# Edge loop of a graph network: four rotating one-bank PSUM tiles in place of two two-bank tiles

## The chip, the cores and the metric

The kernel runs on one core of a Trainium2 chip. The metric is the device time of one execution, in microseconds (us); the median of three runs before the change is 1214.6 us. The engines are named as in the profile: PE is TensorE (PEld its weight loads), DVE is VectorE, ACT is ScalarE, POOL is GpSimd and SP is SyncE.

## What is computed

One layer of message passing over 6250 nodes of 128 features and 100000 edges that are sorted by destination, then a residual and a layer norm:

```python
row, col = (edge_index[0], edge_index[1])
msg_in = jnp.concatenate([node_features[row], node_features[col]], axis=-1)
h = jax.nn.relu(msg_in @ Wm1 + bm1)
h = jax.nn.relu(h @ Wm2 + bm2)
messages = h @ Wm3 + bm3
agg = jax.ops.segment_sum(messages, col, num_segments=num_nodes)
count = jax.ops.segment_sum(jnp.ones((messages.shape[0],), messages.dtype), col, num_segments=num_nodes)
agg = agg / jnp.clip(count, 1.0)[:, None]
node_in = jnp.concatenate([node_features, agg], axis=-1)
upd = jax.nn.relu(node_in @ Wn1 + bn1) @ Wn2 + bn2
...
x = _layernorm(x + _L0_gnn_ref(...), axis=-1)
```

## The kernel before

It has three stages. The first makes two tables in device memory, one row a node: `atab`, the source half of the first product, in float32, and `btab`, the destination half, in three bfloat16 terms. The second, the edge loop, is nearly the whole time. The third applies the node network and the norm.

The edge loop takes the edges in groups of 512 (four tiles of 128), two groups at a time: 196 groups, so 98 pairs. Each group's destinations fall into few nodes, so a one-hot product over a narrow window of nodes sums them. A pair passes through these parts, which overlap with those of its neighbours (in step p of the loop, different pairs are at different parts):

- `fetch`: POOL issues eight indirect gathers of `atab` rows into the tile `rows` (L437); SP issues the loads of the `btab` windows (L443). `rows` has two buffers, so the gathers of pair p+2 wait until the first layer of pair p has read its own.
- `make_hot`: DVE builds one-hot tiles, `oht` (L461) and `oh` (L464).
- `first_layer`: PE transposes the gathered rows (L478) and adds the destination terms (L485) into the tile `ph`, which takes four of the eight PSUM banks; ACT makes `h1` of it (L491).
- `second_layer`: PE multiplies `h1` by `w2` (L499), eight matmuls a group; DVE takes the maximum with the negated bias into `h2` (L503), in one instruction of 128x1024 for the first group of a pair and two of 128x512 for the second (`cuts`). The bias itself is added later, per node.
- `sums`: PE multiplies the one-hot tiles by `h2`, which gives a sum per node of each window (L511); `part_of` copies it to SBUF on ACT (L519; L522 for the short last pair).
- `turned` and `add_up`: PE transposes these sums (L533), and DVE adds each window, 21 nodes wide, into the accumulator `acc` at an offset that it reads at run time (L542), eight adds a pair.

The order on PE, ACT and DVE is the order in which the code is written (`manual_schedule`). In step p PE runs `turned` of pair p-3, `first_layer` of p, `sums` of p-2 and `second_layer` of p-1. DVE runs `add_up` of p-3, `make_hot` of p+1 and the maxima of p-1. ACT runs the activations of p and the copy of p-2. In a few steps a piece of other work is put between: some blocks of the node part (`x_part`, L327, with evictions L329 and L331) in the first two steps and the last but one, and a doubling of the inputs (L567 on DVE, with its loads and stores on SP).

The other four PSUM banks are the pool `p2`. Everything but the first layer takes its tile there. A tile is two banks and there are two of them:

```python
def banks():
    return p2.tile([P, 2, 2 * H], F32, name="banks")

def bank():
    return banks()[:, 0, :].rearrange("p (t h) -> p t h", t=2)
```

One step takes four such tiles: `pt` in `turned`, `pg` in `sums`, and `ph2` twice in `second_layer`. Whoever takes a tile waits until the last reader of the tile that had the buffer before is done with all of it, and a reader waits until all that was written to its tile, in the region that it reads or in the same banks, is there. Which buffer a tile gets is settled when the program is built.

Of the kernel before, what the change touches and what calls it, by code (L numbers as in the profile page):

```python
# [19 lines left out]
P = 128  # L20
EPS = 1e-5
NONE = 16384
WN = 32
# [4 lines left out]
def kernel(  # L28
# [121 lines left out]
    with tc.tile_pool(name="prep", bufs=1) as prep, tc.tile_pool(  # L150
# [183 lines left out]
        def whole(steps):  # L334
            for _ in steps:
                pass
# [75 lines left out]

    with edge, tc.tile_pool(name="wk", bufs=2) as wk, tc.tile_pool(
        name="p1", bufs=1, space=PSUM
    ) as p1, tc.tile_pool(name="p2", bufs=2, space=PSUM) as p2:


        NH2 = 2
# [1 line left out]
        for t in h2s:  # L420
            nc.vector.memset(t[:, :, H:], 1.0)

        def banks():
            return p2.tile([P, 2, 2 * H], F32, name="banks")

        def bank():
            return banks()[:, 0, :].rearrange("p (t h) -> p t h", t=2)

        def fetch(groups):

# [22 lines left out]
        def hot(groups):  # L453


            ohts = wk.tile([P, 2, 2, P], BF16, name="oht")
            ohs = []
            for i, (db, pb_cols, dl, nt) in enumerate(groups):
                n = nt * WN
                for k in range(2):  # L460
                    nc.vector.tensor_scalar(ohts[:n, i, k, :], db[:n, k * P:(k + 1) * P], pb_cols[:n, k:k + 1], None,  # L461
                                            op0=ALU.is_equal)
                oh = wk.tile([P, GT, WN], F32, name="oh", bufs=6)
                nc.vector.tensor_tensor(oh[:, :nt, :], iota_n.to_broadcast([P, nt, WN]),  # L464
                                        dl.rearrange("p (j o) -> p j o", o=1).to_broadcast([P, nt, WN]),
                                        op=ALU.is_equal)
                ohs.append(oh)
            return ohts, ohs
# [23 lines left out]
                                         ph[:, i, :nh, c, :], AF.Relu, bias=b1[:, c:c + 1])  # L492
            return h1

        def second_layer(h1, h2, nt, cuts):
            ph2 = banks().rearrange("p b (t h) -> p (b t) h", t=2)
            for j in range(nt):
                for c in range(HC):
                    nc.tensor.matmul(ph2[:, j, :], h1[:, c, j * P:(j + 1) * P],  # L499
                                     w2[:, c, :], start=(c == 0), stop=(c == HC - 1))  # L500
            step = nt // cuts
            for j in range(0, nt, step):
                nc.vector.tensor_tensor(h2[:, j:j + step, :H], ph2[:, j:j + step],  # L503
                                        nb2.to_broadcast([P, step, H]), op=ALU.max)

        def sums(groups):

            pg = banks()
            for i, (oh, h2, nt) in enumerate(groups):
                for j in range(nt):  # L510
                    nc.tensor.matmul(pg[j * WN:(j + 1) * WN, i, :H + 1], oh[:, j, :], h2[:, j, :],  # L511
                                     start=True, stop=True, skip_group_check=True)
            return pg

        def part_of(pg, nts):
            part = wk.tile([P, 2, H + 1], F32, name="part")
            if min(nts) == GT:
                n = len(nts)
                nc.scalar.copy(part[:, :n], pg[:, :n, :H + 1])  # L519
            else:  # L520
                for i, nt in enumerate(nts):
                    nc.scalar.copy(part[:nt * WN, i], pg[:nt * WN, i, :H + 1])  # L522
            return part

        def turned(part, nts):

            pt = banks()[:, :, :2 * (HC + 1) * NQ].rearrange("p h (g c q) -> p h g c q", g=2, q=NQ)
            for i, nt in enumerate(nts):
                for c in range(HC + 1):
                    for h in range(nt // 2):  # L530
                        rows = (part[halves[h], i, c * P:(c + 1) * P] if c < HC
                                else part[halves[h], i, H:].to_broadcast([NQ, P]))
                        nc.tensor.matmul(pt[:, h, i, c, :], rows, ident[halves[h], halves[h]], is_transpose=True,  # L533
                                         start=True, stop=True, skip_group_check=True)
            return pt

        def add_up(pt, firsts, nts):
            for i in reversed(range(len(nts))):
                for j in reversed(range(nts[i])):
                    window = acc[:, :, ds(firsts[i][j], WB)]  # L540
                    k = j % 2 * WN
                    nc.vector.tensor_add(window, window, pt[:, j // 2, i, :, k:k + WB])  # L542
                    yield

        def load_bases(ap, n, engine):
            _, firsts = nc.values_load_multi_w_load_instructions(
# [42 lines left out]
        for i in range(NP + 4):  # L589
            if i == 8:  # L590
                late_loads()

                none = wk.tile([16, (NG * GE - E) // 16 + 1], I32, name="none", bufs=1)
                nc.vector.memset(none, NONE)
                nc.sync.dma_start(dpad[E - 16:].rearrange("(p e) -> p e", p=16), none)
                nc.sync.dma_start(dpad[:E].rearrange("(p e) -> p e", p=16), dst.rearrange("(p e) -> p e", p=16))
            if i < NP:
                dbs = early.pop(0) if early else destinations(2 * i, min(2, NGF - 2 * i), dst_row)
                if 2 * i + 1 == NGF:
                    dbs = dbs + last_destinations()  # L600
                got = fetch([(srcT[:, 2 * i + k, :], firsts) for k, firsts in enumerate(bases(i, ENG.SP))])
                st[i] = dict(nts=NTS[2 * i:2 * i + 2], got=got, dbs=dbs)
            p = i - 1
            if p < 0:
                continue
            if p == 0:
                make_hot(0)
            k = p - 3
            firsts = bases(k, ENG.DVE) if k >= 0 else None
            if k >= 0:  # L610
                pt = turned(st[k]["part"], st[k]["nts"])
                whole(add_up(pt, firsts, st.pop(k)["nts"]))
            for step, after in enumerate((10, 12, 14)):
                if i >= after and (i - after) % 4 == 0 and (i - after) // 4 < len(pieces):
                    double((i - after) // 4, step)
            if p + 1 < NP:
                make_hot(p + 1)
            if p < NP:
                s = st[p]
                s["h1"] = first_layer(s.pop("got"), s.pop("ohts"), s["nts"])  # L620
            if p < 2:
                whole(x_part(X_FIRST[p], bank, (nc.scalar, nc.vector)))
            if p - 2 == NP - 1:
                whole(rest)
            if 0 <= p - 2 < NP:
                st[p - 2]["part"] = part_of(summed(p - 2), st[p - 2]["nts"])
            if 0 <= p - 1 < NP:
                s = st[p - 1]
                for j, nt in enumerate(s["nts"]):
                    second_layer(s["h1"][:, j], h2s[j], nt, 1 + j)  # L630
        assert not st
        turns.close()
        order.close()
# [7 lines left out]
        with tc.For_i(0, groups, 1) as g:  # L641
            more = nc.values_load(
                morei[0:1, ds(g, 1)], min_val=0, max_val=N // 16,
                skip_runtime_bounds_check_because="the difference of two nodes over 16")
            with tc.For_i(0, more, 1):
                for t, by in ((tilei[0:1, ds(g * GT, GT)], float(WB)), (pbase[:, ds(g, 1), :], float(WB)),
                              (dloc[:, ds(g, 1), :], -float(WB))):
                    nc.vector.tensor_scalar(t, t, by, None, op0=ALU.add)
                idx = wk.tile([P, GT], I32, name="idx")
                nc.vector.tensor_copy(idx, srcT[:, ds(g, 1), :].rearrange("p o j -> p (o j)"))  # L650
                pbc = wk.tile([P, 2], F32, name="pbc")
                nc.vector.tensor_copy(pbc, pbase[:, ds(g, 1), :].rearrange("p o k -> p (o k)"))
                dl = wk.tile([P, GT], F32, name="dl")
                nc.vector.tensor_copy(dl, dloc[:, ds(g, 1), :].rearrange("p o j -> p (o j)"))

                ti = wk.tile([1, GT], I32, name="ti")
                nc.vector.tensor_scalar_min(ti, tilei[0:1, ds(g * GT, GT)], float(N - 1))
                got = fetch([(idx, load_bases(ti, GT, ENG.SP))])
                db, = destinations(g, 1, dpad_row)
                ohts, (oh,) = hot([(db, pbc, dl, GT)])  # L660
                h1 = first_layer(got, ohts, [GT])
                second_layer(h1[:, 0], h2s[0], GT, 1)
                part = part_of(sums([(oh, h2s[0], GT)]), [GT])
                whole(add_up(turned(part, [GT]), [load_bases(ti, GT, ENG.DVE)], [GT]))


    NB = 4 * P
# [159 lines left out]
```

## Time and profile before

| | |
|---|---|
| median of 3 runs | 1214.6 us (1214.6 to 1215.05) |
| profiled execution | 1215.59 us; span of its instructions 1213.9 us |
| granted PE clock, mean | 0.992 |
| PE busy | 1139.8 us, 94% of the span |
| POOL busy | 803.9 us (66%), of it 751.6 us in the gathers (L437), 959 ns each |
| DVE busy | 651.5 us (54%) |
| ACT busy | 381.9 us (31%) |
| edge loop, first L499 to last add | 96.1 to 1136.7 us |

The profile shows one execution. Times in a timeline are microseconds from the start of the span: the start, the duration, the engine, the line of the code, the operation, the tiles as output<-input, and in brackets the idle time of the engine before it and what ended that. A row can merge several instructions of a kind (x32). A float32 matmul that is no transpose shows as two records. A waits row gives who waited for whom, the sum in us, how often and the longest.

### The profile page before, as it was taken

The numbers are of one execution on the slowest core, as the hardware profiler recorded it, in microseconds if no ns is written. First come the engines' busy times: TensorE is split into PE (matmuls) and PEld (weight loads), VectorE is DVE, ScalarE is ACT, GpSimd is POOL, SyncE is SP. The second block draws the span as 40 slices with busy tenths as digits, with TensorE's granted clock in tenths as the row PEclk, the third lists the DMA queues.
The fourth block names the chain that finished last, engine by engine and source line by source line (L and its number), as shares of the span: only waits on it lengthen the run. The fifth ranks groups of instructions, "written<-read, shape, count | busy, mean of one in ns | idle before, by whom it ended". The sixth has DMA issues, their size and how long they took to land. (4 is left out here: it accounts for less than half of the span.)

```text
span 1213.9 us, 31892 instructions
## 1 busy us (share of the span) xinstructions
PE 1139.8 (94%) x11196; PEld 909.9 (75%) x11197; DVE 651.5 (54%) x1978; ACT 381.9 (31%) x679; POOL 803.9 (66%) x862
## 2 busy tenths in 40 slices
PE   7989999999999999999999999999999999998897
PEld 6747777787777777877777778777777787776465
DVE  5764455455555555555555544455455444554587
ACT  5753222222222222222222222222222222221256
POOL 5557777777777777777777777777777777770120
PEclk9999999999999999999999999999999999999899
DMA  8776656566565555556655555555555555550243
GB/s 277 277 253 172 172 165 170 156 173 171 151 171 165 162 152 169 171 160 163 168 157 150 156 156 152 154 153 152 146 148 149 153 154 153 153 147 20 84 117 111
DMA packets 173727, 193.61 MB, mean 160 GB/s; under 512 B 30906, under 2 KB 145548, under 8 KB 173548
## 3 DMA queue, kind: packets, MB, share of 16 engines
q0 software_dynamic: 38160, 103.75, 30.7%
q1 hardware_dynamic: 106956, 61.93, 17.5%
q10 hardware_dynamic: 28448, 25.87, 7.3%
q8 instruction: 89, 1.46, 0.5%
q14 instruction: 74, 0.61, 0.2%
HBM read 168.92 MB, written 22.88 MB: 158 GB/s over the span
## 5 line engine op out<-in xcount | busy, mean ns | idle before, releaser
L437 POOL DMA_INDIRECT rows<-atab,srcT x784 | 751.6, 959 | 281.0 <-issue 189.8
L499 PE MATMUL banks<-w,h 128*128 128x256 f32 x3128 | 698.6, 381 | 45.8 <-DVE acc L542 43.0
L499 PEld LDWEIGHTS banks<-w,h 128*128 128x128 f32 x3128 | 586.2, 190 | 165.8 <-PE banks L511 86.2
L503 DVE TENSOR_TENSOR h<-banks,nb 128x512 f32<-128x512 f32 (+1 forms) x294 | 245.7, 864 | 477.3 <-PE banks L499 471.4
L491 ACT ACTIVATE h<-ph,b 128x512 f32<-128x512 f32 x392 | 236.7, 686 | 744.1 <-PE ph L485 728.4
L542 DVE TENSOR_TENSOR acc<-acc,banks 128x63 f32 x782 | 171.6, 219 | 31.8 <-PE banks L533 5.8
L478 PE MATMUL ph<-ident,rows 64*128 64x64 f32 x3128 | 113.8, 223 | 0.6 <-issue 0.6
L478 PEld LDWEIGHTS ph<-ident,rows 64*128 64x128 f32 x3128 | 105.3, 139 | 2.3 <-ACT x_sb L329 1.3
L511 PE MATMUL banks<-h,oh 128*32 128x257 f32 x1564 | 105.3, 386 | 1.0 <-DVE acc L542 1.0
L461 DVE TENSOR_SCALAR oht<-db,pbase 128x128 bf16<-128x128 int32 x392 | 95.7, 291 | 0.2
L708 POOL TENSOR_TENSOR agg<-total,rc 128x512 f32<-128x512 f32 (+2 forms) x15 | 16.0, 1070 | 81.5 <-DMA rcol<-acc 44.4
L533 PEld LDWEIGHTS banks<-ident,part 64*128 64x128 f32 x1173 | 43.3, 137 | 33.2 <-issue 31.8
L485 PE MATMUL ph<-oht,rows 64*128 64x128 bf16 x1564 | 61.1, 216 | 3.4 <-DMA rows<-btab 3.2
L511 PEld LDWEIGHTS banks<-h,oh 128*32 128x32 f32 x1564 | 40.9, 109 | 28.8 <-PE banks L533 1.1
L519 ACT COPY part<-banks 128x514 f32<-128x514 f32 x97 | 58.6, 604 | 9.9 <-PE banks L511 9.9
L533 PE MATMUL banks<-ident,part 64*128 64x64 f32 x1173 | 56.7, 229 | 0.5 <-ACT part L522 0.5
L464 DVE TENSOR_TENSOR oh<-iota_n,dloc 128x128 f32<-128x128 f32 x196 | 55.2, 282 | 0.4 <-PE banks L511 0.4
L235 PE MATMUL pbt<-w,xT 128*128 128x256 f32 x196 | 49.7, 397 | 4.4 <-ACT bt L244 1.7
L485 PEld LDWEIGHTS <-rows 64*128 64x128 bf16 x1564 | 48.9, 95 | 4.2 <-DMA rows<-btab 4.1
L235 PEld LDWEIGHTS pbt<-w,xT 128*128 128x128 f32 x196 | 36.1, 195 | 14.1 <-ACT bt L244 3.5
L703 PE MATMUL pmt<-acc,w 128*128 128x512 f32 (+2 forms) x60 | 26.1, 576 | 3.2 <-DVEq L641 3.2
L731 PEld LDWEIGHTS pot<-wu,u 128*128 128x128 f32 (+1 forms) x196 | 24.0, 191 | 5.1 <-issue 4.5
(112 smaller groups left out, 412.3 us busy)
## 6 DMA issues: line engine op xcount, KB each, us to landing
rows<-btab SPq DMA_DIRECT2D x782, 32.0 KB
db<-in_dst_dram ACTq DMA_DIRECT2D x194, 128.0 KB
rows<-atab,srcT POOLq DMA_INDIRECT x784
btab<-bt SPq DMA_DIRECT2D x24, 384.0 KB
atab<-bt SPq DMA_DIRECT2D x24, 256.0 KB
xd<-in_x_dram SPq DMA_DIRECT2D x12, 256.0 KB
x2tab<-xd SPq DMA_DIRECT2D x12, 256.0 KB
x_sb<-in_x_dram SPq DMA_DIRECT2D x5, 512.0 KB
```

The source lines that it names most:

```text
L235: nc.tensor.matmul(pbt[:, a, :], xT[:, (t0 + a) * P:(t0 + a + 1) * P], w1[:, k, :], start=True, stop=True)
L437: nc.gpsimd.indirect_dma_start(out=ag[:, j, :], out_offset=None, in_=atab[:, :], in_offset=bass.IndirectOffsetOnAxis(ap=idx[:, j:j + 1], a ...
L461: nc.vector.tensor_scalar(ohts[:n, i, k, :], db[:n, k * P:(k + 1) * P], pb_cols[:n, k:k + 1], None, op0=ALU.is_equal)
L478: nc.tensor.matmul(ph[:, i, h, c, u * NQ:(u + 1) * NQ], ag[halves[h], u, c * P:(c + 1) * P], ident[halves[h], halves[h]], is_transpose=Tru ...
L485: nc.tensor.matmul(ph[:, i, h, c, k * P:(k + 1) * P], bw[halves[h], k, c * P:(c + 1) * P], ohts[halves[h], i, k, :], start=False, stop=Tru ...
L491: nc.scalar.activation(h1[:, i, c, :nh * 2 * P].rearrange("p (h e) -> p h e", h=nh), ph[:, i, :nh, c, :], AF.Relu, bias=b1[:, c:c + 1])
L499: nc.tensor.matmul(ph2[:, j, :], h1[:, c, j * P:(j + 1) * P], w2[:, c, :], start=(c == 0), stop=(c == HC - 1))
L503: nc.vector.tensor_tensor(h2[:, j:j + step, :H], ph2[:, j:j + step], nb2.to_broadcast([P, step, H]), op=ALU.max)
L511: nc.tensor.matmul(pg[j * WN:(j + 1) * WN, i, :H + 1], oh[:, j, :], h2[:, j, :], start=True, stop=True, skip_group_check=True)
L519: nc.scalar.copy(part[:, :n], pg[:, :n, :H + 1])
L533: nc.tensor.matmul(pt[:, h, i, c, :], rows, ident[halves[h], halves[h]], is_transpose=True, start=True, stop=True, skip_group_check=True)
L542: nc.vector.tensor_add(window, window, pt[:, j // 2, i, :, k:k + WB])
```

## The change

`p2` gets four buffers of one bank. `second_layer` takes one tile for each two edge tiles, so four a pair, each with a maximum of 128x512 of its own; `sums` takes one tile a group, and ACT copies each group's sums by itself; `turned` takes one tile for each half `h` (which held one bank of the tile before, too), and `add_up` goes through the first half's windows and then the second's, where it went backwards through groups and windows. `oh` gets eight buffers instead of six. The arithmetic is the same; the order of the adds is not. A step now takes eight tiles from four buffers. The lines below L415 move by up to five: L499 becomes L500, L503 L502, L511 L510, L519 and L522 L518, L533 L529 and L542 L539.

```diff
-    ) as p1, tc.tile_pool(name="p2", bufs=2, space=PSUM) as p2:
+    ) as p1, tc.tile_pool(name="p2", bufs=4, space=PSUM) as p2:
...
-        def banks():
-            return p2.tile([P, 2, 2 * H], F32, name="banks")
-
         def bank():
-            return banks()[:, 0, :].rearrange("p (t h) -> p t h", t=2)
+            return p2.tile([P, 2, H], F32, name="bank")
+
+        def flat_bank():
+            return bank().rearrange("p t h -> p (t h)")
...
-                oh = wk.tile([P, GT, WN], F32, name="oh", bufs=6)
+                oh = wk.tile([P, GT, WN], F32, name="oh", bufs=8)
...
-        def second_layer(h1, h2, nt, cuts):
-            ph2 = banks().rearrange("p b (t h) -> p (b t) h", t=2)
-            for j in range(nt):
-                for c in range(HC):
-                    nc.tensor.matmul(ph2[:, j, :], h1[:, c, j * P:(j + 1) * P],
-                                     w2[:, c, :], start=(c == 0), stop=(c == HC - 1))
-            step = nt // cuts
-            for j in range(0, nt, step):
-                nc.vector.tensor_tensor(h2[:, j:j + step, :H], ph2[:, j:j + step],
-                                        nb2.to_broadcast([P, step, H]), op=ALU.max)
+        def second_layer(h1, h2, nt):
+            for j0 in range(0, nt, 2):
+                ph2 = bank()
+                for j in range(j0, j0 + 2):
+                    for c in range(HC):
+                        nc.tensor.matmul(ph2[:, j - j0, :], h1[:, c, j * P:(j + 1) * P],
+                                         w2[:, c, :], start=(c == 0), stop=(c == HC - 1))
+                nc.vector.tensor_tensor(h2[:, j0:j0 + 2, :H], ph2, nb2.to_broadcast([P, 2, H]), op=ALU.max)
 
         def sums(groups):
 
-            pg = banks()
-            for i, (oh, h2, nt) in enumerate(groups):
+            pgs = []
+            for oh, h2, nt in groups:
+                pg = flat_bank()
                 for j in range(nt):
-                    nc.tensor.matmul(pg[j * WN:(j + 1) * WN, i, :H + 1], oh[:, j, :], h2[:, j, :],
+                    nc.tensor.matmul(pg[j * WN:(j + 1) * WN, :H + 1], oh[:, j, :], h2[:, j, :],
                                      start=True, stop=True, skip_group_check=True)
-            return pg
-
-        def part_of(pg, nts):
+                pgs.append(pg)
+            return pgs
+
+        def part_of(pgs, nts):
             part = wk.tile([P, 2, H + 1], F32, name="part")
-            if min(nts) == GT:
-                n = len(nts)
-                nc.scalar.copy(part[:, :n], pg[:, :n, :H + 1])
-            else:
-                for i, nt in enumerate(nts):
-                    nc.scalar.copy(part[:nt * WN, i], pg[:nt * WN, i, :H + 1])
+            for i, (pg, nt) in enumerate(zip(pgs, nts)):
+                nc.scalar.copy(part[:nt * WN, i], pg[:nt * WN, :H + 1])
             return part
 
         def turned(part, nts):
 
-            pt = banks()[:, :, :2 * (HC + 1) * NQ].rearrange("p h (g c q) -> p h g c q", g=2, q=NQ)
+            pts = [flat_bank()[:, :2 * (HC + 1) * NQ].rearrange("p (g c q) -> p g c q", g=2, q=NQ) for _ in range(2)]
             for i, nt in enumerate(nts):
                 for c in range(HC + 1):
                     for h in range(nt // 2):
...
-                        nc.tensor.matmul(pt[:, h, i, c, :], rows, ident[halves[h], halves[h]], is_transpose=True,
+                        nc.tensor.matmul(pts[h][:, i, c, :], rows, ident[halves[h], halves[h]], is_transpose=True,
                                          start=True, stop=True, skip_group_check=True)
-            return pt
-
-        def add_up(pt, firsts, nts):
-            for i in reversed(range(len(nts))):
-                for j in reversed(range(nts[i])):
-                    window = acc[:, :, ds(firsts[i][j], WB)]
-                    k = j % 2 * WN
-                    nc.vector.tensor_add(window, window, pt[:, j // 2, i, :, k:k + WB])
-                    yield
+            return pts
+
+        def add_up(pts, firsts, nts):
+            for h in range(2):
+                for i in range(len(nts)):
+                    for j in range(2 * h, min(2 * h + 2, nts[i])):
+                        window = acc[:, :, ds(firsts[i][j], WB)]
+                        k = j % 2 * WN
+                        nc.vector.tensor_add(window, window, pts[h][:, i, :, k:k + WB])
...
-                    second_layer(s["h1"][:, j], h2s[j], nt, 1 + j)
+                    second_layer(s["h1"][:, j], h2s[j], nt)
```

## The prediction

> **What bounds the kernel now.** I read the page's first part for the engine with the most work, then the waits, then the timeline of one step in the middle, one step near the start and the steps at the end.
>
> ```profile
> PE 1139.8 (94%) x11196; PEld 909.9 (75%) x11197; DVE 651.5 (54%) x1978; ACT 381.9 (31%) x679; POOL 803.9 (66%) x862
> ```
>
> TensorE (PE) is busy for 94% of the span, so the question is what its few idle microseconds wait for. The list of waits answers:
>
> ```profile
> POOL rows L437 <- issue: 189.8, 621, 0.6
> ...
> POOL rows L437 <- PE ph L485: 59.6, 80, 1.0
> ...
> PE banks L499 <- DVE acc L542: 43.0, 94, 0.9
> ```
>
> In 94 of the 98 steps the second layer's first matmul (L499) waits for the last window add of VectorE (DVE, L542), 43.0 us in all: its two-bank tile is the one from which the adds still read. GpSimd (POOL), which gathers rows (L437), waits for PE only 80 times; the rest of its idle time is a fixed 0.30 us between gathers. The timeline of one step (start, duration, engine, line) shows both:
>
> ```profile
> 608.97 0.58 PE L533 MATMUL banks<-ident,part 64*128 64x64 f32 x12
> 609.08 1.29 DVE L503 TENSOR_TENSOR h<-banks,nb 128x512 f32<-128x512 f32 x2 [2.23 <-PE banks L499]
> ...
> 609.39 1.16 PE L478 MATMUL ph<-ident,rows 64*128 64x64 f32 x32
> ...
> 610.28 2.00 DVE L542 TENSOR_TENSOR acc<-acc,banks 128x63 f32 x8
> ...
> 610.38 0.61 PE L485 MATMUL ph<-oht,rows 64*128 64x128 bf16 x16
> ...
> 610.92 1.07 PE L511 MATMUL banks<-h,oh 128*32 128x257 f32 x16
> ...
> 611.27 0.95 POOL L437 DMA_INDIRECT rows<-atab,srcT  x1 [0.78 <-PE ph L485]
> ...
> 612.42 7.14 PE L499 MATMUL banks<-w,h 128*128 128x256 f32 x32 [0.43 <-DVE acc L542]
> ...
> 613.39 0.60 ACT L519 COPY part<-banks 128x514 f32<-128x514 f32 x1
> ...
> 619.50 0.58 PE L533 MATMUL banks<-ident,part 64*128 64x64 f32 x12
> ```
>
> The step lasts 619.50 - 608.97 = 10.53 us. By the starts: L533 to L478 0.42, L478 to L485 0.99, L485 to L511 0.54, L511 to L499 1.50, L499 to the next L533 7.08. The adds start late (610.28) because DVE first does both maxima of the step before, 609.08 to 610.37; and those began only when all eight matmuls of that two-bank tile were done. An early step that has no adds shows the same passage without the wait:
>
> ```profile
> 104.76 1.07 PE L511 MATMUL banks<-h,oh 128*32 128x257 f32 x16
> ...
> 105.76 7.17 PE L499 MATMUL banks<-w,h 128*128 128x256 f32 x32
> ```
>
> L511 to L499 takes 1.00 there, not 1.50. The wait therefore costs 0.50 per step: its 0.43 to 0.46 of idle time and a slower restart.
>
> **The change, part by part.**
>
> *Finer release of the adds' bank.* One step has eight one-bank tiles in four buffers: two for the transposes, two for the sums, four for the second layer. In the built order the four second-layer tiles reuse, in 94 steps, the two transpose banks and then the two sums banks. Set time 0 at L533. The last maximum still starts at 0.11, but is one of 0.69 instead of two, so DVE is free at 0.80 instead of 1.40. Eight adds take 2.00, 0.25 each, and the new order serves bank h=0 first: it is free at 1.8, the other at 2.8. PE wants them at 0.42 + 0.99 + 0.54 + 1.00 = 2.95 and, a quarter of 7.08 later, at 4.72. The wait goes, with 1.1 us to spare. PE's own step becomes 10.03, and 94 x 0.50 = 47.0 us is what PE alone would gain, with 0.4 more at the first such tile, which waited for the node-part evictions.
>
> *What is late next inside the step.* The third and fourth tiles, at 6.49 and 8.26, need ScalarE's (ACT) copies of the sums. The copy starts at 613.39 - 608.97 = 4.42 and becomes two of 0.37 (the 128x257 copies at the kernel's end, L522, take 368 to 375 ns) instead of one of 0.60: done at 4.8 and 5.2. The sums at 1.95 need the last maximum, done at 0.80. None of these is late.
>
> *More, smaller instructions.* DVE does four maxima of 0.69 for one of 1.22 and two of 0.69, that is 0.15 per step or 14.6 us busy; ACT gains 2 x 0.37 - 0.60 = 0.14, or 13.6 us. I charge nothing: before its maxima DVE idles 471.4 us waiting for L499, and ACT idles 728.4 us before the first layer's activations. Without that cover it would be 28 us. Two more buffers of the one-hot tile take away a wait of 0.4 us in the whole run: nothing.
>
> *More waits on PE's queue.* The built order has eight cross-engine waits on these tiles per step instead of four. No row prices a wait that is satisfied early by itself. One bound is zero: inside the 32 matmul records of L499 the second tile's first matmul already waits for the copy, and 7.14 us for 32 is an even 0.22 each. The other is 0.33, the idle time of the weight loads ahead of L533 (31.8 us in 96), which waits for a maximum long past. A gain from a wait is excluded. I take zero, from the row on the same instruction.
>
> *GpSimd.* This is the end that PE meets. Its gathers start every 1.26 us (0.953 + 0.303), 8 per pair of groups: 10.06, against PE's 10.53 now and 10.03 after. So PE catches up and POOL takes over. Its fastest run: the 25th gather starts at 100.33 and 759 follow to the last of 784; 759 x 1.257 = 954.1, plus 0.95 for the last and some 3.3 for 15 gathers that take about 1.17 to 1.28 (one at 623.05 beside DVE's L567): the last ends at 1058.7, instead of 1095.9. The last L478 needs those rows. In the windows after 1095.9 the DMA traffic stops between 1098 and 1099, so the rows land 2.4 us after the issue, and the last tile is first read 0.7 after L478 begins: L478 can start 1.7 to 2 after the issue ends, at the earliest. The smallest lead that the trace holds without a stall is 3.2 (pair 3: gathers end 110.08, L478 at 113.28). L478 of the last pair thus starts at 1060.5 to 1061.9, say 1061. PE alone would be there at 113.28 - 0.4 + 94 x 10.03 = 1055.7. The later one counts: 1105.9 - 1061 = 45 us saved up to there.
>
> *The end of the edge loop.* Here the two-bank tiles make four more stalls:
>
> ```profile
> 1110.14 7.17 PE L499 MATMUL banks<-w,h 128*128 128x256 f32 x32 [1.62 <-ACT part L519]
> ...
> 1118.79 1.07 PE L511 MATMUL banks<-h,oh 128*32 128x257 f32 x16 [0.97 <-DVE acc L542]
> ...
> 1120.61 5.45 PE L499 MATMUL banks<-w,h 128*128 128x256 f32 x24 [0.75 <-ACT part L519]
> ...
> 1128.88 1.13 PE L327 MATMUL banks<-xT,wu 128*128 128x512 f32 x2 [0.78 <-ACT x_sb L329]
> ```
>
> In the first of these the new order waits for a copy only at the second tile, 1.8 us later, when it is done: 1.6 gained. In the next step the first group's sums no longer wait for the second group's maximum, and the second layer waits for one group's copy: 0.97 + 0.75 = 1.7. The four node-part matmuls (L327) had one buffer at a time to turn over and have two: from L533 at 1125.99 to L511 at 1132.69 is 6.7 now; four evictions of 0.69 behind a first matmul need some 3.7. That is 3.0. Sum 6.3, between 2 (the chain only shifts onto ACT) and 7; I take 6.
>
> *Sum.* The profiled execution took 1215.59 (span 1213.9), about 1.0 above the median of 1214.6. 1215.6 - 45 - 6 = 1164.6, less the 1.0: **1164 us**.
>
> *A rule against it.* PE's granted clock is 1.00 in every window from 96 to 1136 us, with one idle gap of 0.43 per step. I keep 1.00, since the gaps shrink. The Trainium skill's page "TensorE: Matmul & The Clock Gate", section "A second HAM failure mode: psum-queue depth-cycling", says that cycling through PSUM banks each iteration can leave small idle gaps between matmul groups that throttle the clock again and again; this change cycles twice as often. By that rule, a tenth of the 98 x 7.08 us of L499 at half rate would add an estimated 69 us, and the sum would be 1233; no row shows it.
>
> **The rivals.**
>
> *PE takes it all.* If gathers ran faster than 10.06 per pair, 47.4 + 6 gives 1161. Against it: 0.30 between gathers even when POOL waits for nothing.
>
> *Half of it.* If POOL needs its present lead (last gather to L478: 10.0 us) and the tail gives nothing, only POOL's own 37.2 go: 1177. For it: after pair 17 the lead has never been small. Against it: early pairs run at 3.2 without a stall.
>
> *Slower: the waits stop the weight loads.* If each of the four new waits per step cost PE the 0.33 seen ahead of L533, that is 4 x 97 x 0.33 = 128 us against 51 gained: 1291. It decides from 51 / 388 = 0.13 us per wait. Against it: the even 0.22 inside L499, and PE itself shows no idle time before L533.
>
> *It does nothing.* If another wait stood behind the adds (the copies, the maxima), the time stays at 1214. Against it: 1.00 in the early step.
>
> **How the numbers follow.** Forecast 0.63, PE takes it all 0.13, half of it 0.15 (all three faster), slower 0.07, nothing 0.02. Low end: 1161 less 5 for a tail and restart cost that I set too small, 1156. High end: 1177 and 3 for longer gathers under denser traffic, 1180; this leaves out the slow case, the empty one and strays, under 2 in 10. Faster by over 0.2% (about what a measurement of this kernel can tell from no change) 0.91, within 0.2% 0.02, slower 0.07.
>
> **What would show it.** Right: no wait of L500 (the new L499) for the adds; a step of about 10.06; POOL's gathers 0.30 apart throughout, with almost no wait for PE; late in the loop small PE waits at L478 for gathered rows; the edge loop's tail some 6 us shorter. Wrong: idle time at L500 for ACT copies, matmul spacing above 0.22 inside L500, gathers above 0.96, a granted clock under 1.00, or a step still near 10.5.

## The result, and the profile after

The changed kernel takes 1164.14 us in the median of four runs (1163.3 to 1167.19) against 1214.6 us before (1214.5 to 1215.05): a ratio of 0.9588, with a 95% interval of 0.957 to 0.9607. The profiled execution took 1164.89 us, its span is 1163.2 us and its mean granted PE clock 0.992, as before. The prediction was 1164. Ratios, here and below, leave out runs that took over 1.5% longer than the fastest of the same kernel.

The page of the changed kernel, engine by engine (busy time, share of the span, instructions):

```profile
PE 1136.6 (98%) x11196; PEld 910.8 (78%) x11197; DVE 687.6 (59%) x2075; ACT 388.0 (33%) x776; POOL 801.9 (69%) x862
```

PE does the same work in a span that is 50.7 us shorter: its share goes from 94% to 98%. DVE and ACT do more, and PE doesn't wait for it in the rows below. The list of waits (who waited for whom: sum, times, longest) and the groups by line (busy time, mean ns of one, idle time before):

```profile
POOL rows L437 <- issue: 207.6, 681, 0.3
PEld bank L500 <- PE bank L510: 39.7, 96, 0.5
DVE acc L539 <- DVE h L502: 33.3, 89, 0.7
```

```profile
L437 POOL DMA_INDIRECT rows<-atab,srcT x784 | 750.1, 957 | 246.4 <-issue 207.6 <-DMA rows<-atab,srcT 12.5 <-DMA rows<-btab 9.7
L500 PE MATMUL bank<-w,h 128*128 128x256 f32 x3128 | 701.2, 382 | 0.1
...
L478 PE MATMUL ph<-ident,rows 64*128 64x64 f32 x3128 | 115.6, 223 | 2.3 <-DMA rows<-atab,srcT 1.5 <-issue 0.6
```

The row of 43.0 us, in which L499 waited for the adds, has no successor: all 3128 matmul records of L500 together have 0.1 us of idle time before them. The row in which POOL waited 80 times for PE is gone as well; what is left before a gather is almost wholly the fixed 0.3. A new row is DVE's own: the adds (L539) wait for a maximum (L502), 33.3 us. One step of the changed kernel, from its timeline:

```profile
576.94 0.58 PE L529 MATMUL bank<-ident,part 64*128 64x64 f32 x12
577.05 0.69 DVE L502 TENSOR_TENSOR h<-bank,nb 128x512 f32<-128x512 f32 x1 [1.03 <-PE bank L500]
...
577.36 1.16 PE L478 MATMUL ph<-ident,rows 64*128 64x64 f32 x32
577.46 0.95 POOL L437 DMA_INDIRECT rows<-atab,srcT  x1 [0.30 <-DMA rows<-atab,srcT]
578.10 2.08 DVE L539 TENSOR_TENSOR acc<-acc,bank 128x63 f32 x8 [0.36 <-DVE h L502]
...
578.35 0.61 PE L485 MATMUL ph<-oht,rows 64*128 64x128 bf16 x16
...
578.89 1.07 PE L510 MATMUL bank<-h,oh 128*32 128x257 f32 x16
...
579.90 7.17 PE L500 MATMUL bank<-w,h 128*128 128x256 f32 x32
...
581.36 0.66 ACT L518 COPY part<-bank 128x257 f32<-128x257 f32 x2
581.93 0.70 DVE L502 TENSOR_TENSOR h<-bank,nb 128x512 f32<-128x512 f32 x1 [0.57 <-PE bank L500]
...
587.00 0.58 PE L529 MATMUL bank<-ident,part 64*128 64x64 f32 x12
```

The step lasts 587.00 - 576.94 = 10.06 us, and no PE line of it carries a wait. L510 to L500 is 1.01, where it was 1.50. The first maximum of the next step starts at 581.93, two microseconds into L500, and no longer after eight matmuls.

At the end of the edge loop, where four stalls stood before:

```profile
1061.82 1.03 PE L478 MATMUL ph<-ident,rows 64*128 64x64 f32 x22
...
1064.35 7.17 PE L500 MATMUL bank<-w,h 128*128 128x256 f32 x32
...
1073.16 5.45 PE L500 MATMUL bank<-w,h 128*128 128x256 f32 x24
1078.54 0.58 PE L529 MATMUL bank<-ident,part 64*128 64x64 f32 x12
1079.05 3.89 PE L327 MATMUL bank<-xT,wu 128*128 128x512 f32 x8
1082.87 1.06 PE L510 MATMUL bank<-h,oh 128*32 128x257 f32 x12
```

The eight records of the four node-part matmuls now run as one row of 3.89 us; before there were three rows with 0.43, 0.78 and 0.78 of idle time.

### The profile page after: what moved, and what is told of

Same layout as the page of the kernel before. It is cut to its first block, busy times and chain, and to the rows that moved or that the text cites. A ratio compares the mean times of both kernels' runs of the same rounds, so it can differ in the third digit from the quotient of the medians.

```text
span 1163.2 us, 32186 instructions
## 1 busy us (share of the span) xinstructions
PE 1136.6 (98%) x11196; PEld 910.8 (78%) x11197; DVE 687.6 (59%) x2075; ACT 388.0 (33%) x776; POOL 801.9 (69%) x862
## 5 line engine op out<-in xcount | busy, mean ns | idle before, releaser
L500 PE MATMUL bank<-w,h 128*128 128x256 f32 x3128 | 701.2, 382 | 0.1
L500 PEld LDWEIGHTS bank<-w,h 128*128 128x128 f32 x3128 | 586.2, 190 | 116.1 <-PE bank L510 39.7
L502 DVE TENSOR_TENSOR h<-bank,nb 128x512 f32<-128x512 f32 x391 | 270.8, 693 | 350.4 <-PE bank L500 334.8
L539 DVE TENSOR_TENSOR acc<-acc,bank 128x63 f32 x782 | 172.8, 221 | 72.0 <-DVE h L502 33.3
L478 PE MATMUL ph<-ident,rows 64*128 64x64 f32 x3128 | 115.6, 223 | 2.3 <-DMA rows<-atab,srcT 1.5
L478 PEld LDWEIGHTS ph<-ident,rows 64*128 64x128 f32 x3128 | 106.0, 139 | 5.0 <-DMA rows<-atab,srcT 2.5
L510 PE MATMUL bank<-h,oh 128*32 128x257 f32 x1564 | 105.2, 386 | 0.0
L461 DVE TENSOR_SCALAR oht<-db,pbase 128x128 bf16<-128x128 int32 x392 | 99.4, 313 | 1.0 <-DMA db<-in_dst_dram 1.0
L529 PEld LDWEIGHTS bank<-ident,part 64*128 64x128 f32 x1173 | 43.2, 136 | 32.9 <-issue 32.2
L518 ACT COPY part<-bank 128x257 f32<-128x257 f32 x196 | 65.2, 401 | 6.7 <-PE bank L510 6.7
L510 PEld LDWEIGHTS bank<-h,oh 128*32 128x32 f32 x1564 | 40.9, 109 | 27.9 <-ACT x_sb L329 0.8
L529 PE MATMUL bank<-ident,part 64*128 64x64 f32 x1173 | 56.7, 229 | 0.1
```

Source lines behind the costliest of these rows:

```text
L478: nc.tensor.matmul(ph[:, i, h, c, u * NQ:(u + 1) * NQ], ag[halves[h], u, c * P:(c + 1) * P], ident[halves[h], halves[h]], is_transpose=Tru ...
L500: nc.tensor.matmul(ph2[:, j - j0, :], h1[:, c, j * P:(j + 1) * P], w2[:, c, :], start=(c == 0), stop=(c == HC - 1))
L502: nc.vector.tensor_tensor(h2[:, j0:j0 + 2, :H], ph2, nb2.to_broadcast([P, 2, H]), op=ALU.max)
L510: nc.tensor.matmul(pg[j * WN:(j + 1) * WN, :H + 1], oh[:, j, :], h2[:, j, :], start=True, stop=True, skip_group_check=True)
L518: nc.scalar.copy(part[:nt * WN, i], pg[:nt * WN, :H + 1])
L529: nc.tensor.matmul(pts[h][:, i, c, :], rows, ident[halves[h], halves[h]], is_transpose=True, start=True, stop=True, skip_group_check=True)
```

## The experiments

The question was which part of the change frees PE. Theory A is the prediction's: the new order of the adds, which serves one bank completely before the other, together with a last maximum that is half as long. The rivals are that one of these alone does it, or neither. Each of the next four kernels is the changed kernel with one piece undone, beside 1215.6 us for the kernel before (1213.92 to 1216.79, seven runs on the same chip).

**The old order of the adds.**

```diff
-            for h in range(2):
-                for i in range(len(nts)):
-                    for j in range(2 * h, min(2 * h + 2, nts[i])):
+            for i in reversed(range(len(nts))):
+                for j in reversed(range(nts[i])):
...
-                        nc.vector.tensor_add(window, window, pts[h][:, i, :, k:k + WB])
+                    nc.vector.tensor_add(window, window, pts[j // 2][:, i, :, k:k + WB])
```

> The new kernel with the old order of the window adds (backwards through groups and windows), so that the bank of the first half is free only after the eighth add instead of the fourth. In the new kernel's trace the adds run from 1.16 to 3.24 us after the first transpose and the second layer wants that bank at 2.95. Theory A (the order of the adds frees the bank in time): a wait of about 0.4 us is back before the second layer in 94 steps, some 1200 us, and the profile names the adds again. Rival B (one-bank tiles and the earlier maximum are enough, as the numbers of the prediction, adds done at 2.8, would have it): no wait, 1164 us.

Measured: 1164.87 us (1163.38 to 1166.53), ratio 0.9584 (0.9568 to 0.96). The whole gain stays, so theory A falls in this point. In the groups by line of this kernel the second layer still waits for nothing:

```profile
L500 PE MATMUL bank<-w,h 128*128 128x256 f32 x3128 | 701.0, 382 | 0.6
```

**Both maxima of a group after its last matmul**, as before, in reverse order:

```diff
+            made = []
             for j0 in range(0, nt, 2):
                 ph2 = bank()
...
+                made.append((j0, ph2))
+            for j0, ph2 in reversed(made):
                 nc.vector.tensor_tensor(h2[:, j0:j0 + 2, :H], ph2, nb2.to_broadcast([P, 2, H]), op=ALU.max)
```

> The new kernel with the two maxima of each group taken in reverse order, so that both wait for the group's last matmul, as they did with the two-bank tile. The adds then start at about 1.3 and the first bank is free at 2.3, the second at 3.3; they are wanted at 2.95 and 4.7. Theory A: nothing changes, 1164 us within 3. Rival B (the gain comes from the maxima that end earlier): the old wait is back, up to 47 us, some 1205 us.

Measured: 1165.8 us (1162.59 to 1167.07), ratio 0.958 (0.9562 to 0.9597): the early maxima alone are not needed either.

**Both undone**, that is the two edits above together. What is left of the change is that tiles are of one bank, the copies by group and the two `oh` buffers:

> Old order of the adds and late maxima together, in the one-bank tiles. Theory A: the wait of before, 0.45 to 0.5 us per step, is back: 1164 + 94 x 0.45 = some 1207 us, little more than the old order of the adds alone. Rival B: the two effects only count together, so this is the first of the three to be slower. If the tiles' size itself made the gain, in whatever order: 1164 us.

Measured: 1164.61 us (1163.9 to 1165.89), ratio 0.9582 (0.9566 to 0.9598). The adds now run exactly when they ran in the kernel before, and still PE doesn't wait. From the timeline of this kernel (the second layer is L501 here, the transposes L532, the maxima L505, the sums L513, the adds L541):

```profile
585.22 0.58 PE L532 MATMUL bank<-ident,part 64*128 64x64 f32 x12
585.32 1.29 DVE L505 TENSOR_TENSOR h<-bank,nb 128x512 f32<-128x512 f32 x2 [2.16 <-PE bank L501]
...
586.53 2.00 DVE L541 TENSOR_TENSOR acc<-acc,bank 128x63 f32 x8
...
587.17 1.07 PE L513 MATMUL bank<-h,oh 128*32 128x257 f32 x16
...
588.17 7.17 PE L501 MATMUL bank<-w,h 128*128 128x256 f32 x32
```

The adds run from 1.31 to 3.31 us after the transposes begin, as they did before (1.31 to 3.31). Before, L499 had to wait for the eighth of them: they ended at 612.28 and it began at 612.42, 0.14 later. Here L501 begins at 588.17, with adds running until 588.53. The handing out of buffers, which is settled when the program is built, explains it: the first second-layer tile gets the buffer that is released first. With the old order that is the bank of the second half, whose last reader is the sixth add, at 586.53 + 6 x 0.25 = 588.03, again 0.14 before L501 begins. The bank that the eighth add releases at 588.53 goes to the second tile, wanted at 588.17 + 7.1 / 4 = 589.9. In the changed kernel the same first tile takes the bank that the fourth add releases. The traces bear this out. In PE's queue the wait for VectorE ahead of the second layer's first matmul ends 0.09 us after the sixth add in all 94 steps of this kernel; it ends 0.09 after the fourth add in 90 steps of the changed kernel, and 0.09 after the eighth in all 94 of the kernel before. So two tiles with a release each are enough, and neither the order of the adds nor the early maxima is. The two leave room (the fourth add is done some 0.8 us before L500 begins) where this kernel has none: in one step L501 does wait for the adds, 0.6 us.

**Six buffers of `oh`**, the one edit that I had costed at nothing:

```diff
-                oh = wk.tile([P, GT, WN], F32, name="oh", bufs=8)
+                oh = wk.tile([P, GT, WN], F32, name="oh", bufs=6)
```

> The new kernel with six buffers of the one-hot tile instead of eight. The wait that this brings back cost 0.4 us in the whole run before: 1164 us within 2. Rival: with the shorter step DVE meets the sums that still read the tile and the time rises by more than 5 us.

Measured: 1163.0 us (1162.92 to 1164.67), ratio 0.9565 (0.9549 to 0.9581): nothing.

The runs that follow fell on three other chips, on which the kernel before takes 1680 to 1768 us and PE's mean granted clock is 0.84 to 0.90; only kernels of one chip are compared, and sizes don't carry over to the first chip. The last section says what was different there.

**Splitting only one part.** With four banks, one tile of two banks and two of one: in the first kernel the transposes and the first group's second layer share the two-bank tile, in the second the sums and the second group's second layer do. If the separate release of the transposes' halves is what frees PE, the first must show the wait and the second must not.

```diff
-    ) as p1, tc.tile_pool(name="p2", bufs=4, space=PSUM) as p2:
+    ) as p1, tc.tile_pool(name="p2", bufs=1, space=PSUM) as p2, tc.tile_pool(name="p3", bufs=2, space=PSUM) as p3:
...
+        def pair():
+            return p2.tile([P, 2, 2 * H], F32, name="pair")
...
-            pts = [flat_bank()[:, :2 * (HC + 1) * NQ].rearrange("p (g c q) -> p g c q", g=2, q=NQ) for _ in range(2)]
+            both = pair()
+            pts = [both[:, h, :2 * (HC + 1) * NQ].rearrange("p (g c q) -> p g c q", g=2, q=NQ) for h in range(2)]
...
-                    second_layer(s["h1"][:, j], h2s[j], nt)
+                    second_layer(s["h1"][:, j], h2s[j], nt, j == 0)
```

`bank()` takes from `p3`; with the last argument true, both tiles of a group are halves of one `pair()` and their maxima come after its last matmul. The second kernel takes `pair()` in `sums` and passes `j == 1`.

> One part undone: the transposes of the sums and the first group's second layer share one two-bank tile again, as before; the sums and the second group's second layer keep one-bank tiles. The first matmul of the second layer then needs all eight adds, whichever order they have. In the new kernel's trace these end 3.24 us after the first transpose, and the matmul is wanted at 2.95. Theory A' (a tile per half lets the planner give out the bank that comes free first): a wait of 0.3 to 0.4 us is back in 94 steps, 1164 + 94 x 0.37 = some 1199 us, with the adds named as releaser. Rival E (the gain is in the sums and the maxima, which keep their new form here): 1164 us.

> The other part undone: the sums and the second group's second layer share one two-bank tile, with that group's two maxima only after its last matmul; the transposes and the first group's second layer have one-bank tiles. Theory A': the adds start at 1.3 and a bank is free by 2.4, so the steps stay at 10.06 and the time is 1164 us, up to 5 more at the end of the edge loop. Rival E: the wait for the adds is back, some 1205 us.

Measured, beside 1683.64 us for the kernel before on that chip: 1687.11 us (1674.53 to 1705.53), ratio 0.9998 (0.9951 to 1.0044), with the transposes in the pair, and 1642.17 us (1630.17 to 1650.09), ratio 0.9711 (0.9639 to 0.9783), with the sums in it. The waits of PE for the adds, first kernel (L505 is the second layer, L549 the adds):

```profile
PE pair L505 <- DVE acc L549: 14.0, 16, 1.7
```

In the second kernel, L505 waits for no add. So the wait comes back when the halves of the transposes share a tile, though in 16 steps and not in the 94 expected, and stays away when they don't. The expected times were worked out for the first chip and say nothing here, and the size is not settled. The 14.0 us are a third of the 45 us between the two kernels, on a chip that has other waits than the first.

**Which engine sets the step of 10.06.** One gather of eight replaced by a plain load of the same size (its rows are then not the ones asked for), or one of the second layer's matmuls left out (second group, last tile, the second half of the sum over features), or both:

```diff
+                    if i == 1 and j == GT - 1:
+                        nc.sync.dma_start(ag[:, j, :], atab[:P, :])
+                        continue
```

```diff
-                    for c in range(HC):
+                    n = 1 if short and j == GT - 1 else HC
+                    for c in range(n):
```

> The new kernel unchanged, as the measure for the three beside it: 1164 us within 2.

> The new kernel in which one of a pair's eight gathers is a plain load of 128 rows, issued by SP: GpSimd's pair takes 8.8 us instead of 10.06. It leaves out the gathering of a quarter of the second group's source rows. Theory A (GpSimd sets the pace, PE is just behind it): PE goes on at its own step, 3 to 6 us are gained, and the lead of the gathers grows back to some 9 us. Rival C (PE alone sets the pace): below 1 us. Rival D (GpSimd sets it by far): 10 us or more.

> The new kernel in which one matmul of the second layer in each pair is left out (half of the contraction for one of the eight edge tiles): PE's step is 0.44 us shorter. Theory A (GpSimd sets the pace): 1 to 3 us gained, and PE waits at L478 for gathered rows in nearly every step. Rival C (PE alone sets it): 94 x 0.44 = 41 us gained.

> Both of these: one gather a pair made a plain load, and one matmul a pair left out. Theory A: now neither is in the way, and the step falls to PE's 10.06 - 0.44 = 9.62: some 41 to 45 us gained. If a third thing (the DMA queues, DVE, the landing of the rows) stands close behind, less than 30 us.

> The new kernel in which one matmul of the second layer in each pair is left out (half of the contraction for one of the eight edge tiles): PE's step is 0.44 us shorter. Theory A (GpSimd's gathers set the pace, PE is just behind): 1 to 3 us gained against 1164, and PE waits at L478 for gathered rows in nearly every step. Rival C (PE alone sets the pace): 94 x 0.44 = 41 us gained.

> The same, and one of a pair's eight gathers is a plain load of 128 rows issued by SP (it leaves out the gathering of a quarter of the second group's source rows), so GpSimd's pair takes 8.8 us. Theory A: the step falls to PE's 10.06 - 0.44 = 9.62 and 41 to 45 us are gained against 1164. If something third (the DMA queues, DVE, the landing of the rows) stands close behind, less than 30 us.

Measured on one chip (before: 1679.59): the changed kernel 1665.13 us, ratio 0.9935 (0.9897 to 0.9972); a gather less 1536.0, ratio 0.9144 (0.9085 to 0.9204); a matmul less 1676.82, ratio 1.0001 (0.9969 to 1.0034); both 1534.13, ratio 0.9171 (0.9117 to 0.9226). On another (before: 1768.1): a matmul less 1723.39, ratio 0.975 (0.971 to 0.9789); both 1575.48, ratio 0.8924 (0.8871 to 0.8977). The gather is worth 129 to 148 us on these two chips and the matmul nothing that can be counted on. That answers for a step of 15.2 us (the mean there), not for one of 10.06: which engine sets the pace on the first chip stays open by experiment.

## Why the prediction was right, point by point

- **The wait for the adds goes.** Right, from 43.0 us to none. The account of it was too rich: I let the new order of the adds and the shorter last maximum carry it, and three runs show that PE is freed without either, by the two separate tiles. I had not seen that the order in which buffers are released also decides which tile gets which, so that the old order is served too: its sixth add is done before PE needs the bank, with late maxima only just.
- **The adds' times.** Wrong, without effect. They run from 1.16 to 3.24 after L529, not from 0.80 to 2.80: DVE idles 0.36 between the last maximum and the first add, 33.3 us in 89 steps. In the runs where both maxima come together that idle time is missing (there the adds begin at 586.53, and the maxima that began at 585.32 took 1.29). In the built order the loads of the windows' offsets stand behind that maximum, which waits for PE; that the loads are the 0.36 is argued, not shown. The first bank is free at 2.1, when the fourth add ends, before 2.95.
- **PE's step.** 10.06, not 10.03: L500 to the next L529 takes 7.10 (7.08 forecast), L510 to L500 1.01 (1.00), the rest as forecast. The mean step from pair 3 to the last is 10.10, from 10.56.
- **POOL's pace.** The time is right: the last gather ends at 1058.05 (1058.7 forecast), a pair takes 10.06. But "POOL takes over" is not shown, and that 1061 came out is partly luck. From pair 3's L478 at 112.73 to the last pair's at 1061.82 PE took 949.1 us for 94 steps, and stood idle for gathered rows in 1.5 of them. The rest, 947.6, is 10.08 a step. So PE by itself would have been there at some 1060.3, not at the 1055.7 of the prediction, which took 10.03 for every step; GpSimd's end, which the sum went by, happened to lie beside it. The rows' lead over PE, which was 10.0 us before, is 2.0 at pair 40, and there PE doesn't wait; at the last pair it is 3.8, so the last L478 did not wait for its rows either. The two engines are within some 0.03 us of each other per step. The forecast of 45 us up to there came out as 1105.91 - 1061.82 = 44.1.
- **More instructions on DVE and ACT.** Covered, as said, though DVE's share was mis-sized: the maxima take 270.8 us instead of 245.7, 25 more and not 14.6, since two that follow each other take 1.29 and a single one 0.69. ACT's two copies take 0.66 together; ACT is busy 6.1 us more in all (388.0 against 381.9), not 13.6.
- **More waits on PE's queue.** Nothing: L500's 32 records take 7.17 us, as in the early step before, with a wait on each of its four tiles. The rival that priced each at 0.33 would have shown 1291.
- **The tail.** From the last L478 to the last add 24.5 us instead of 30.8: 6.3 against a forecast of 6. The parts were 1.6 + 1.7 + 3.0 forecast; they measured 1.70 (1061.82 to 1064.35 against 1105.91 to 1110.14), 1.66 (between the last two L500s, 8.81 against 10.47) and 2.37 (L529 to L510, 4.33 against 6.70), and the last 0.57 came from after that, most of it in the short last pair (L510 to L529, 1.19 against 1.60).
- **The clock.** The granted clock is 1.00 in every window from 100 to 1058 us. The Trainium skill's page "TensorE: Matmul & The Clock Gate" warns in its section on psum-queue depth-cycling that turning over banks each iteration can throttle the clock by small gaps; eight turned-over tiles a step did nothing of the kind here, and the estimate of 69 us by that rule is not borne out.

The sum 1215.6 - 45 - 6 = 1164.6 became 1215.59 - 44.1 - 6.3 - 0.3 (after the edge loop) = 1164.89.

## What to carry to other kernels

Where a two-bank tile is read piece by piece and the next writer wants only one bank, look at what its last reader holds up: a tile for each bank gives back the first half while the second is still being read, and the cost of twice as many waits and of smaller evictions is small where their engines idle. Before a gain is booked, put every engine's own step beside the new one: here the gathers need 10.06 us a pair, as much as PE now takes for a step, so a larger gain on PE alone would have met them. The order of the readers decides which half comes free first, and a buffer planner may already make use of that, so don't credit an order that was never tried alone.

## What the runs showed of the hardware

The same kernel can run in another regime on another chip. On one of the three chips above (where it takes 1665.13 us), the changed kernel's profile has PE busy for 80% of the span at a granted clock of 0.869, gathers of the same 0.95 us at the same 0.30 distance, and a step of 15.2 us in the mean. The timeline of the changed kernel there:

```profile
796.63 7.17 PE L500 MATMUL bank<-w,h 128*128 128x256 f32 x32
...
804.89 0.96 POOL L437 DMA_INDIRECT rows<-atab,srcT  x1 [0.30 <-issue]
805.49 0.69 DVE L502 TENSOR_TENSOR h<-bank,nb 128x512 f32<-128x512 f32 x1 [6.75 <-remote]
...
807.67 1.89 DVE L502 TENSOR_TENSOR h<-bank,nb 128x512 f32<-128x512 f32 x3 [1.49 <-remote]
808.41 0.44 PEld L529 LDWEIGHTS bank<-ident,part 64*128 64x128 f32 x11 [2.04 <-DVE h L502]
...
811.65 1.32 POOL L437 DMA_INDIRECT rows<-atab,srcT  x1 [5.80 <-PE ph L485]
```

The first maximum should follow L500's start by 2 us and comes 8.9 us after it; the others follow in a burst, at 0.6 us from each other instead of 1.73. Their idle time carries the label "remote", which names no engine. In the median of 70 steps the last maximum begins 2.97 us after the last gather of a pair has been issued (one in ten under 2.4, one in ten over 3.3), and in the step above DMA traffic stops at about 807.3 and the burst begins at 807.67. By this timeline a ring closes: the gathers (10.06 us), the held-up maxima, PE's transposes and first layer, and the gathers again, which had to wait for it (5.80 above). One gather less takes the pair from 15.21 to 13.91 in the mean, 1.30 less, about its pitch of 1.26. After this hold PE's clock is granted at half, by the windows of the same profile (length, busy time of PE, PEld, DVE, ACT and POOL, granted clock, DMA share, GB/s):

```profile
804.00:808.00 4.00, 0.27 (x1) 0.14 (x1) 1.03 (x2) 0.00 (x0) 1.54 (x2) 1.00 0.33 101
808.00:809.00 1.00, 0.58 (x18) 0.59 (x20) 1.00 (x3) 0.00 (x0) 0.00 (x0) 1.00 0.00 0
809.00:812.00 3.00, 3.00 (x55) 2.50 (x55) 2.69 (x10) 0.53 (x1) 0.35 (x1) 0.52 0.00 0
```

The half clock follows the idle stretch, so it is not what starts it. What holds up the maxima while gathers run on these chips, and not on the first, is not shown by any run here; nor is it why the kernel with the sums in the two-bank tile gains more against the kernel before than the whole change does (0.9711 and 0.9935, each on a chip of its own).
